# A two-layer convolution and linear-attention kernel: key tiles of 128 places in a row instead of every fourth column

## The chip, the cores and the metric

The kernel runs on one core of a Trainium2 chip. The metric is the time of one execution on the device in microseconds (us); the median of several runs is given. A core has five engines that each work through their own instructions in order and wait for each other through semaphores: TensorE (matrix products; in the profile PE for the matmuls and PEld for the loads of their stationary operand), VectorE (DVE), ScalarE (ACT), GpSimd (POOL) and SyncE (SP), which here issues all DMAs.

## The reference, cut to what matters

The input x has 16 batches of 256 channels, 64 rows and 64 columns, all in f32. Layer 0 adds to x a grouped 3x3 convolution of the normalized x, whose weights are rotated and modulated batch by batch. Layer 1 is linear attention over the N = 4096 places with a 5x5 depthwise convolution of v beside it:

```python
xt = x.reshape(B, C, N).transpose(0, 2, 1)
q = xt @ Wq.T + bq
kv = xt @ Wkv.T + bkv
k, v = (kv[..., :C], kv[..., C:])
...
z = 1.0 / (jnp.einsum('bic,bc->bi', q, k.sum(axis=1)) + 1e-06)
kv_state = jnp.einsum('bjc,bjd->bcd', k, v)
out = jnp.einsum('bic,bcd->bid', q, kv_state) * z[..., None]
fm = v.transpose(0, 2, 1).reshape(B * nh, hd, num, num)
fm = lax.conv_general_dilated(fm, dwc_w, window_strides=(1, 1), padding=[(KERNEL_SIZE // 2, KERNEL_SIZE // 2)] * 2, dimension_numbers=('NCHW', 'OIHW', 'NCHW'), feature_group_count=hd) + dwc_b[None, :, None, None]
```

Between these lines q and k are made positive, cubed and scaled back to their norm, place by place. The sums over j (all places) in `k.sum` and `kv_state` don't depend on the order of the places. The depthwise convolution does: it needs v by rows and columns.

## The kernel before

**Tiles.** After layer 0 a batch's x lies on chip as 8 tiles of 512 places (8 rows of 64), channels on partitions in two halves. The keys and values are made in 32 tiles of 128 places, places on partitions. A step n (`key_step`) makes tiles 2n and 2n+1; four tiles, two steps, share one tile of x. A product needs two matmuls, one for each half of the channels, and each f32 matmul of the program stands as two loads and two matmuls in the trace, so a tile has four and a step eight. Line 524 takes every fourth place of the 512 (`T % BC:CH:BC` with BC = 4 and CH = 512), that is, every fourth column of eight rows.

**From keys to state.** VectorE adds the bias (L493), takes the maximum with a small number (L494) and writes v into one of six buffers (L533). ScalarE squares the keys and sums the squares (L500), GpSimd cubes them (L503), ScalarE squares again, VectorE divides the two sums (`ratio`, L508 and L509), GpSimd takes the root (`root`, L512), and ScalarE scales the keys (`key_scale`, L544). `values` (L557) then multiplies keys and values into the state in small 128x32 products, 32 a key step. Step n calls ratio, root and key_scale for n-2, and every second step calls values for two earlier steps.

**v for the convolution.** `key_store` writes v of step n-1 at the end of step n into `vpad` in device memory. vpad has four planes, one for each column modulo 4; a plane holds, row by row, 16 columns of 256 numbers. `load_blocks` (L579) reads it back in an order that the depthwise product (L594) wants, 16 transfers for each half of the image: the first half in steps 7 to 14, the second during the attention. vpad is there twice, by even and odd batch.

**Order.** It is written out by hand (`tc.manual_schedule()`). For each batch come the key steps (the first three of a batch run inside the attention of the one before), then `between`, which starts the convolution of the next batch's layer 0 (`convolve`, L355, unit 0, whose rows `load_rows` fetched in step 11 as `xr`, L334 and L339), finishes the values and does the first half of the depthwise product, then 17 attention steps of 256 places. The preparation of a later batch's layer-0 weights (`prepare`, among it L266, L274, L286, L294) is handed out in pieces over the key steps. All DMAs go through SyncE in program order: stores and loads of v, xr, x for statistics (L97), weights and the output (L698). Eight semaphores tell of their landing, taken in turn.

**PSUM.** Six banks (`bank`) are shared by all products but the state's.

Of the kernel before, what the change touches and what calls it, by code (L numbers as in the profile page):

```python
# [15 lines left out]
P = 128  # L16
# [4 lines left out]
NH, HD = 8, 32  # L21
CH = 512
NCH = N // CH
NT = N // P
ROWS = CH // W
# [9 lines left out]
BR, BC = 8, 4  # L35
# [4 lines left out]
NV = 6  # L40
# [10 lines left out]
def conv_attention(ctx: ExitStack, tc: tile.TileContext, x, consts, kw, b1, w2, b2, b2r,  # L51
                   wkv, wq, brow, srow, wp, bp, dwb, band, out):
    nc = tc.nc
# [24 lines left out]
    def bank(name):  # L78
        return ps.tile([P, CH], F32, tag="bank", name=name)
# [4 lines left out]
    state = {}  # L84
# [57 lines left out]
    vbuf = []  # L142
# [254 lines left out]
    for name, src, bsrc in (("kv", wkv, brow[C:3 * C]), ("q", wq, brow[0:C])):  # L397
        n = src.shape[1]
        w = xp.tile([P, 2, n], F32, tag="x", name=f"wl{name}")
# [26 lines left out]
    for (w, br), lo in zip(wl.values(), (0, 2 * C)):  # L426
# [3 lines left out]
        n = w.shape[2]  # L430
# [11 lines left out]
    vpad = [dcp.tile([BC, H + 4, NJ, C], F32, tag=f"vpad{n}", name=f"vpad{n}") for n in range(2)]  # L442
# [45 lines left out]
    def focus(r, name):  # L488
        return {"r": r, "name": name, "s": sp.tile([P, 4, 2], F32, tag="s", name=f"s_{name}", bufs=5)}
# [24 lines left out]
    def key_products(b, n, j):  # L514

        w, _ = state[b]["kv"]
        if j == 0:
            r = rp.tile([P, 2, C], F32, tag="r0", name=f"rk_{b}_{n}", bufs=5)
            state[b]["k"][n] = focus(r, f"k_{b}_{n}")
            state[b]["k"][n]["pm"] = []  # L520
        T = 2 * n + j
        pm = bank(f"pk_{b}_{T}")
        for t in range(2):
            nc.tensor.matmul(pm, lhsT=state[b]["x"][n // 2][:, t, T % BC:CH:BC], rhs=w[:, t, :],  # L524
                             start=t == 0, stop=t == 1)
        state[b]["k"][n]["pm"].append(pm)

# [6 lines left out]

    def key_store(b, n):
        for j in range(2):
            k, y = (2 * n + j) % BC, ROWS * (n // 2) + 2
            nc.sync.dma_start(vpad[b % 2][k, y:y + ROWS].rearrange("y j n -> (y j) n"),
                              vbuf[n % NV][:, j, 0:HD, :].rearrange("p c h -> p (c h)"))

    def key_scale(b, n):
        f = state[b]["k"][n]
# [175 lines left out]
    def key_step(b, n, made):  # L718


        k = state[b]["k"]
        key_products(b, n, 0)
        if n >= 2:
            ratio(k[n - 2], False)
            root(k[n - 2])
        if n >= 1:
            squares(k[n - 1], 0)
            cube(k[n - 1])
        if n >= 2:
            key_scale(b, n - 2)  # L730
        key_bias(b, n, 0)
        next(made, None)
        key_products(b, n, 1)
        if n >= 1:
            squares(k[n - 1], 1)
        key_bias(b, n, 1)
        if n == LATE:
            values(b, 0)
        elif n > LATE and n % 2:
            values(b, n - LATE - 1)  # L740
            values(b, n - LATE)
        next(made, None)
# [40 lines left out]
    def attention_step(b, p, chain):  # L783
# [30 lines left out]
        if n >= 0:  # L814
            k = state[b + 1]["k"]
            key_products(b + 1, n, 0)
            key_products(b + 1, n, 1)
            if n == 2:
                ratio(k[0], False)
                root(k[0])  # L820
            if n >= 1:
                squares(k[n - 1], 0)
                cube(k[n - 1])
            key_bias(b + 1, n, 0)
            key_bias(b + 1, n, 1)
# [38 lines left out]
        if n >= 1:  # L864
            key_store(b + 1, n - 1)
# [7 lines left out]
    with tc.manual_schedule():  # L873
        fold_load(0, "q")
        made = iter(())
        for b in range(B):
            more = b + 1 < B
            state[b]["f"], state[b]["xq"] = {}, {}
            for n in range(0 if b == 0 else LEAD, NP):
                if b == 0 and n < 4:  # L880
                    load_stats(1, 2 * n)
                    load_stats(1, 2 * n + 1)
                if b == 0 and n == 4:
                    load_kernels(1)
                    made = prepare(1)
                key_step(b, n, made)
                if b == 0 and n < 4:
                    take_stats(1, 2 * n)
                    take_stats(1, 2 * n + 1)
                if n >= 1:  # L890
                    key_store(b, n - 1)
                if b > 0 and n == LEAD:
                    fold_load(b, "q")
                if n == 5:
                    fold_scale(b, "q")
                if n == 6:
                    fold_shift(b, "q")
                if 7 <= n < 15:
                    load_blocks(b, 2 * n - 14)
                    load_blocks(b, 2 * n - 13)  # L900
                if more and n == 11:
                    load_rows(b + 1, 0)
                if NP - 3 <= n < NP - 1:
                    blocked(b, n - NP + 3)
            key_store(b, NP - 1)
            for _ in made:
                pass
# [88 lines left out]
```

## Time and profile before

| what | value |
|---|---|
| median of 3 runs | 3578.64 us (3578.04 to 3583.35) |
| span of the profiled execution | 3572.8 us |
| VectorE, ScalarE, GpSimd busy | 66%, 56%, 45% |
| DMA moved in the span | 514.58 MB, 144 GB/s |
| DMA engines' time on SyncE's queue | 45.8% of 16 engines' span |
| granted TensorE clock, mean | 0.994 |

The span goes from the first to the last instruction of one profiled execution; a timed run has some microseconds around it. A row of the groups reads: line, engine, operation, what it writes and reads, shape, count, busy time in us, mean time of one in ns, and the idle time of the engine just before with what ended it. Busy time of a group counts overlapping instructions once, so it is less than count times mean for matmuls, which are pipelined; their ends are modelled, their starts are not. Idle time of an engine that doesn't set the pace costs nothing.

### The profile page before, as it was taken

To read this page: it belongs to the slowest core of one execution; us is meant where nothing else is said; L and a number is where in the kernel's file an instruction comes from. 1 tells how busy PE (TensorE), PEld (TensorE's weight loads), DVE (VectorE), ACT (ScalarE), POOL (GpSimd) and SP (SyncE) were. 2 spreads that over 40 slices of the span, in tenths; PEclk is the share of its full clock that TensorE was granted. 3 is DMA by queue.
4 is the path that set the end of the run, shared out by engine and by line. 5 is a ranking of instruction groups with operands and counts; after the bars stand their busy time and mean duration, and the time that the engine had idled before them with its cause. 6 is when DMAs were issued, how large, how long until landed. Compare 5 with 4: busy or idle time off the path is not lost. (4 is left out here: it accounts for less than half of the span.)

```text
span 3572.8 us, 114570 instructions
## 1 busy us (share of the span) xinstructions
PE 3457.5 (97%) x46568; PEld 2681.7 (75%) x46568; DVE 2341.4 (66%) x6627; ACT 2010.2 (56%) x6501; POOL 1623.0 (45%) x1807
## 2 busy tenths in 40 slices
PE   4899999999999999999999999999999999999999
PEld 3577787777877768777786877878778787877878
DVE  4656667666685666756666676666756667566656
ACT  2454655647555565655646546474555656556465
POOL 3344545445353453534545344454544535345445
PEclk9999999999999999999999999999999999999999
DMA  6353552635546254452645526355363544625242
GB/s 182 109 161 115 156 175 100 194 97 176 153 131 183 87 172 148 156 168 81 188 127 162 169 86 193 117 159 176 107 195 97 168 149 149 179 85 170 92 153 96
DMA packets 219857, 514.58 MB, mean 144 GB/s; under 512 B 26645, under 2 KB 99863, under 8 KB 207044
## 3 DMA queue, kind: packets, MB, share of 16 engines
q1 hardware_dynamic: 219332, 507.26, 45.8%
q8 instruction: 368, 6.03, 0.7%
q14 instruction: 157, 1.29, 0.1%
HBM read 371.63 MB, written 135.53 MB: 142 GB/s over the span
## 5 line engine op out<-in xcount | busy, mean ns | idle before, releaser
L524 PE MATMUL pk<-wkv,x 128*128 128x512 f32 x2048 | 957.4, 614 | 0.0
L662 POOL TENSOR_TENSOR o<-o,fm 128x256 f32<-128x256 f32 x512 | 362.1, 728 | 993.0 <-DVE o L660 852.0
L524 PEld LDWEIGHTS pk<-wkv,x 128*128 128x128 f32 x2048 | 616.1, 311 | 203.7 <-issue 2.8
L355 PE MATMUL pc<-xr,wt 32*32 32x504 f32 (+1 forms) x17856 | 623.7, 599 | 15.9 <-DMA xr<-in_x 8.6
L355 PEld LDWEIGHTS pc<-xr,wt 32*32 32x32 f32 x17856 | 387.8, 104 | 217.4 <-issue 101.7
L680 PE MATMUL py<-oT,wp 128*128 128x256 f32 x2048 | 505.9, 390 | 0.9 <-ACT oT L672 0.7
L619 PE MATMUL pq<-wq,xq 128*128 128x256 f32 x2048 | 489.6, 382 | 0.0
L500 ACT ACTIVATE r_k<-rk 128x256 f32<-128x256 f32 x1024 | 416.2, 408 | 112.4 <-POOL rk L503 69.0
L500 ACT ACTIVATE r_q<-rq 128x256 f32<-128x256 f32 x1024 | 413.7, 408 | 79.9 <-DVE rq L494 50.2
L368 ACT ACTIVATE x<-pc,shift 128x512 f32<-128x512 f32 x256 | 165.4, 690 | 442.3 <-PE pc L355 442.3
L680 PEld LDWEIGHTS py<-oT,wp 128*128 128x128 f32 x2048 | 370.0, 190 | 50.9 <-issue 3.6
L619 PEld LDWEIGHTS pq<-wq,xq 128*128 128x128 f32 x2048 | 370.8, 191 | 42.6
L544 ACT ACTIVATE rk<-rk,s_k 128x256 f32<-128x256 f32 x512 | 231.5, 499 | 253.9 <-POOL s_k L512 253.9
L493 DVE TENSOR_TENSOR pq<-pq,bq 128x512 f32<-128x512 f32 x256 | 177.2, 692 | 297.5 <-PE pq L619 297.3
L672 ACT COPY oT<-po 128x512 f32<-128x512 f32 x256 | 149.8, 585 | 391.9 <-PE po L670 391.4
L503 POOL TENSOR_TENSOR rk<-r_k,rk 128x512 f32<-128x512 f32 x256 | 327.5, 1279 | 70.5 <-ACT r_k L500 69.1
L512 POOL TENSOR_TENSOR s_k<-s_k,phalf 128x2 f32<-128x2 f32 x256 | 176.8, 691 | 388.9 <-DVE s_k L509 379.1
L503 POOL TENSOR_TENSOR rq<-r_q,rq 128x512 f32<-128x512 f32 x256 | 327.0, 1277 | 29.9 <-issue 28.1
L512 POOL TENSOR_TENSOR s_q<-s_q,phalf 128x2 f32<-128x2 f32 x256 | 178.9, 699 | 325.2 <-DVE s_q L509 262.4
L493 DVE TENSOR_TENSOR pk<-pk,bkv 128x256 f32<-128x256 f32 x512 | 218.1, 426 | 135.3 <-PE pk L524 133.5
L378 DVE TENSOR_TENSOR x<-x,shift 128x16 f32<-128x16 f32 x256 | 67.9, 265 | 324.0 <-ACT x L368 324.0
L651 PE MATMUL pn<-kvx,qT 128*128 128x132 f32 x2048 | 273.2, 277 | 0.0
(128 smaller groups left out, 5226.8 us busy)
## 6 DMA issues: line engine op xcount, KB each, us to landing
vh<-vpad SPq DMA_DIRECT2D x256, 384.0 KB
vh<-vpad SPq DMA_DIRECT2D x256, 360.0 KB
vpad<-v SPq DMA_DIRECT2D x512, 128.0 KB
out<-x SPq DMA_DIRECT2D x128, 512.0 KB
xr<-in_x SPq DMA_DIRECT2D x186, 320.0 KB
xs<-in_x SPq DMA_DIRECT2D x224, 256.0 KB
xr<-in_x SPq DMA_DIRECT2D x62, 288.0 KB
xs<-in_x SPq DMA_DIRECT2D x16, 512.0 KB
```

The lines of the kernel that those rows point to most:

```text
L355: nc.tensor.matmul(pcs[q].rearrange("p (r w) -> p r w", w=W)[ts(j, HD), :, to:to + n], lhsT=wt[ts(q, HD), j, k, :], rhs=g[ts(q, HD), j, r: ...
L368: nc.scalar.activation(state[b]["x"][i][:, t, :], state[b]["pc"][q], AF.Identity, bias=state[b]["shift"][:, t, 3:4])
L493: nc.vector.tensor_add(pm, pm, bias)
L500: nc.scalar.activation(f["r2"][:, j, :], f["r"][:, j, :], AF.Square, accum_out=f["s"][:, k, j:j + 1])
L503: nc.gpsimd.tensor_mul(f["r"], f["r2"], f["r"])
L512: nc.gpsimd.tensor_tensor(f["s"][:, 3, :], f["s"][:, 2, :], phalf, ALU.pow)
L524: nc.tensor.matmul(pm, lhsT=state[b]["x"][n // 2][:, t, T % BC:CH:BC], rhs=w[:, t, :], start=t == 0, stop=t == 1)
L544: nc.scalar.mul(f["r"][:, j, :], f["r"][:, j, :], f["s"][:, 3, j:j + 1])
L619: nc.tensor.matmul(pq[:, j, :], lhsT=xq[:, t, ts(j, P)], rhs=w[:, t, :], start=t == 0, stop=t == 1)
L651: nc.tensor.matmul(pn[:, :, 4 * hh:4 * hh + 4], lhsT=qT[:, hh, j, :], rhs=kvx[:, hh], start=True, stop=True)
L662: nc.gpsimd.tensor_add(o, o, fm[:, 2 * (m % NCH) + j, :])
L680: nc.tensor.matmul(py[:, co].rearrange("p y (J c) -> p J y c", c=BC), lhsT=wp_t[:, t, ts(co, P)], rhs=oT[:, t, :].rearrange("p (J y c) -> ...
```

## The change

A key tile becomes two whole rows of 64 places: tile T takes the places T % 4 times 128 to that plus 127 of its x tile, words in a row. A partition now stands for a column, the first 64 for one row and the other 64 for the next. So `key_store` writes each tile in two transfers, one a row of the image, from 64 partitions each; a row's 64 places go to the four planes in turn, 1 KB each. Before, a tile went to eight rows of one plane in one transfer from 128 partitions.

```diff
@@ key_products
         for t in range(2):
-            nc.tensor.matmul(pm, lhsT=state[b]["x"][n // 2][:, t, T % BC:CH:BC], rhs=w[:, t, :],
+            nc.tensor.matmul(pm, lhsT=state[b]["x"][n // 2][:, t, ts(T % 4, P)], rhs=w[:, t, :],
                              start=t == 0, stop=t == 1)
@@ key_store
         for j in range(2):
-            k, y = (2 * n + j) % BC, ROWS * (n // 2) + 2
-            nc.sync.dma_start(vpad[b % 2][k, y:y + ROWS].rearrange("y j n -> (y j) n"),
-                              vbuf[n % NV][:, j, 0:HD, :].rearrange("p c h -> p (c h)"))
+            for r in range(2):
+                y = 4 * n + 2 * j + r + 2
+                nc.sync.dma_start(vpad[b % 2][:, y].rearrange("k j n -> j k n"),
+                                  vbuf[n % NV][ts(r, W), j, 0:HD, :].rearrange("p c h -> p (c h)"))
```

`ts(i, n)` is the slice from i times n to (i + 1) times n. What vpad holds in the end is the same, and so is everything that reads it.

## The prediction

> **What bounds the kernel now.** I read the page first: busy time and the costliest groups.
>
> ```profile
> span 3572.8 us, 114570 instructions
> PE 3457.5 (97%) x46568; PEld 2681.7 (75%) x46568; DVE 2341.4 (66%) x6627; ACT 2010.2 (56%) x6501; POOL 1623.0 (45%) x1807
> ...
> L524 PE MATMUL pk<-wkv,x 128*128 128x512 f32 x2048 | 957.4, 614 | 0.0
> L524 PEld LDWEIGHTS pk<-wkv,x 128*128 128x128 f32 x2048 | 616.1, 311 | 203.7 <-issue 2.8
> ...
> L619 PEld LDWEIGHTS pq<-wq,xq 128*128 128x128 f32 x2048 | 370.8, 191 | 42.6
> ```
>
> TensorE is busy 97% of the span, and the key products (L524) are its largest group. Their weight load is the odd one: 311 ns, where the query product, a load of the same 128x128 f32, takes 191. The difference in the program is the step: L524 takes every fourth word of x, L619 words in a row. Whether those 120 ns cost time depends on what covers a load, so next comes TensorE's timeline in batch 1 (start, duration, matmuls merged).
>
> ```profile
> 348.94 0.60 PE L634 MATMUL pt<-consts,rq 128*128 128x128 f32 x4
> 349.38 3.72 PE L524 MATMUL pk<-wkv,x 128*128 128x512 f32 x8
> ...
> 376.25 1.21 PE L557 MATMUL pkv<-v,rk 128*32 128x33 f32 x64
> 377.39 3.82 PE L524 MATMUL pk<-wkv,x 128*128 128x512 f32 x8
> 381.05 1.03 PE L474 MATMUL pbq<-wq,co 128*128 128x256 f32 x4
> 381.91 3.61 PE L524 MATMUL pk<-wkv,x 128*128 128x512 f32 x8
> ...
> 434.09 2.00 PE L619 MATMUL pq<-wq,xq 128*128 128x256 f32 x8
> ...
> 470.79 1.89 PE L619 MATMUL pq<-wq,xq 128*128 128x256 f32 x8
> ```
>
> The same eight key matmuls take 3.61, 3.72 or 3.82 us, by what ran before them. Single starts in the trace say why. Inside a run they are 429 ns apart, and the 311 ns load hides fully under the matmul before. Only the first one of a run shows its load: its distance to the second is 657 ns after the small tiled products (L557, L294, L196, L209), 631 after L168 and L225, 550 after transposes (L634, L670), 443 after L474. So 228, 202, 121 and 14 ns are exposed. For the 191 ns load of the query the same two places show 104 ns after L557 (320 against 216; the 2.00 us row, whose forerunner is L557) and 2 ns after transposes (the 1.89 us row).
>
> **The weight load (L524).** It becomes 128 words in a row, as at L619. Its price is not in the trace for this line; the bounds are 311 (nothing gained) and nothing exposed at all, and I take L619's row, which has the same shape and type. Each entry then loses 228-104 = 124 ns after small products and 121-2 = 119 after transposes; after L168 and L225 I take 119 too, the difference of the loads. TensorE's order of instructions, which stays the same, has 220 runs of L524: 126 after small products, 30 after L168 and L225, 45 after transposes, 17 after L474, two others. Sum: 126 x 0.124 + 75 x 0.119 = 24.5 us of TensorE time. If nothing stayed exposed it would be 126 x 0.228 + 30 x 0.202 + 45 x 0.121 = 40.2 us. Inside the runs nothing changes.
>
> The Trainium skill (TensorE: Matmul & The Clock Gate, LDWEIGHTS (loading the stationary operand)) speaks against this: load time goes by the columns alone, 128 / 1.2 GHz, about 107 ns whatever the layout. By it the edit is worth nothing and the time stays at 3578.6. The rows of 311 and 191 ns for equal columns speak for another term, and I go by the rows.
>
> **How much of it reaches the end.** TensorE is not alone everywhere. I looked for places where it already waits, and found one in the key phase, here in batch 1 (TensorE, then ScalarE, then GpSimd).
>
> ```profile
> 410.82 1.50 PE L557 MATMUL pkv<-v,rk 128*32 128x33 f32 x64
> ```
> ```profile
> 410.91 0.91 ACT L544 ACTIVATE rk<-rk,s_k 128x256 f32<-128x256 f32 x2 [0.70 <-POOL s_k L512]
> ```
> ```profile
> 407.41 1.91 POOL L266 TENSOR_TENSOR rtmp<-mix,kw 128x864 f32<-128x864 f32 x1
> 409.27 0.84 POOL L333 COPY xr<-edge 32x256 f32<-32x256 f32 x2
> 410.19 0.69 POOL L512 TENSOR_TENSOR s_k<-s_k,phalf 128x2 f32<-128x2 f32 x1
> ```
>
> The group of values(9) and values(10) takes 1.50 us where others take 1.20, because key 10's scaled rows are just then being made: in 15 of 16 batches its matmuls start 0.10 us after ScalarE has finished them. The chain behind it is root (GpSimd), scaling and squares (ScalarE), ratio (VectorE), once a step, with the next batch's kernel preparation in between (L266, L333). It does not follow TensorE there: VectorE ends key tile 10 1.3 us after its last matmul, as it does wherever it waits for TensorE, but from tile 14 on 4.1 to 5.6 us after. What TensorE gains between tile 10 and values(10) is waited away at 410.82. That takes four entries in each of batches 1 to 14 (377.39, 386.58, 394.90, 403.63): 4 x 14 x 0.124 = 6.9 us. Batch 0 has a similar chain; I give it 0.4. Entries before tile 10 pull the chain along and are kept; after values(10) two more, 0.25 us, come before values(12), which has 0.3 us of room (0.4 us against the least, 0.1). Batch 15 prepares nothing, VectorE stays at 1.3 us, and all is kept.
>
> Kept: 24.5 - 6.9 - 0.4 = 17.2 us.
>
> **The stores (L534).** Two transfers of 128 KB a key step become four of 64 KB, 512 more on SyncE's queue. The packets stay at 1 KB and as many.
>
> ```profile
> L538 SPq DMA_DIRECT2D vpad<-v x512: 314/325/1470, 118.0 to 3462.0; - x171
> L579 SPq DMA_DIRECT2D vh<-vpad x512: 759/770/1567, 152.3 to 3504.4; - x171
> L448 SPq DMA_DIRECT2D vpad<-zero x16: 303/422/1307, 41.6 to 62.9; - x16
> ```
>
> An issue of the new shape is not in the trace. Bounds: 0.31 us (the least of L538) and 0.77 (L579); nearest is L448, which writes vpad in the same three-dimensional form, 0.42. A step of about 4.15 us then holds 4 x 0.42 + 2 x 0.77 = 3.2 us of issues, before 2 x 0.325 + 2 x 0.77 = 2.2. The queue still waits for VectorE's v, not the reverse. Behind the stores stand the loads of vh, xr and x. The program also gives DMAs eight semaphores in rotation, so each waits for the landing of the eighth before it, and with six a step instead of four that reaches less far back. From the landings around step 11 I estimate up to 1 us for that, so xr comes about 2 us late (1.04 us of issues, 1 of landings). Landing events in the trace put the last of unit 0's four xr 3.3 to 15.7 us (median 6.2) before its first matmul, and the last vh 7.0 us or more before the first-half depthwise. Less the roughly 1.1 us that TensorE gains until then, some 5 us of cover remain at the median and 2.2 at the tightest. Cost: 0. If the cover were gone, TensorE would stand in front of L355 with everything of `between` behind it.
>
> The Trainium skill (SBUF — State Buffer, Can I just issue two DMAs to hit both halves?) says that halves by partition serialize and one transfer of 128 is better. Doubling the stores' packet time by it (256 x 49 ns / 16 = 0.8 us a step) would raise the DMA share in the key phase from 0.72 to 0.91, still covered; the sum would not move.
>
> **VectorE's waits.** In the changed program 291 of the 512 writes of v (L533) wait for two DMAs instead of one, those of six steps earlier. Such a step is 25 us old and the slowest store landed after 12.3, so they don't block, but an extra wait instruction is 21 ns on VectorE. Queued behind it are the next tile's bias and the ratio. Bounds: 0, and 14 x 14 x 0.021 = 4.1 us if all between tile 11 and values(10) lie on the chain. I take 0: in the gating step VectorE itself waited 0.39 us for ScalarE.
>
> **Sum.** The profiled execution: 3572.8 - 17.2 = 3555.6 us of span. The median of the runs, 3578.64, lies 5.8 above that span; so 3561.4, say 3561.
>
> **Rivals.**
> A, everything kept: the chain at values(10) moves along with TensorE. 3578.6 - 24.5 = 3554. For it: TensorE's idle time put down to it is small; against: the same 0.10 us in 15 batches, and tile lags that only preparation explains.
> B, half kept: VectorE's extra waits lie on the chain (4.1 us), and xr is late in the tightest batches (some 2 us more): 3561 + 6 = 3567. The VectorE share of 89% (32.18 of 36 us between 385 and 421) speaks for it, its wait for ScalarE against.
> C, no gain: the load is long for another reason than its step, 3579. Against: L474, also beside 512-column matmuls of the same weights, loads in 191 ns.
> D, slower: the stores clog SyncE's queue, and xr comes late in all 15 batches. At 0.77 us a store, a step's issues are 6 x 0.77 = 4.6 us and the queue falls back 0.5 us a step, 2.5 us from step 7 to 11, about 5 with the step's own; that just uses up the cover. From a delay of 5 + 17.2 / 15 = 6.2 us on the kernel is slower than before; at 8 us it is 3561 + 15 x 3 = 3606. Against: L448's row.
>
> **How the numbers follow.** Forecast 0.65, A 0.12, B 0.09, C 0.06, D 0.08. The forecast's own range is 3557 to 3566. The range of 3552 to 3570 takes in A and B and leaves out C and D. From no change a measurement of this kernel can tell 0.2%, 7.2 us. Faster: forecast, A and B, 0.86; same: C, 0.06; slower: D, 0.08.
>
> **What would show it.** The load at L524 at about 191 ns; eight key matmuls after L557 in about 3.71 us, after transposes in 3.60; L557's group of values(10) longer than 1.50 us, at about 1.9 to 2.0, which shows A wrong; store issues near 0.42 us; no wait of L355 for xr at unit 0. A load still near 311 ns makes the whole forecast wrong; waits for xr or vh on TensorE mean D.

## The result, and the profile after

| kernel | median (runs) | ratio to before, 95% interval |
|---|---|---|
| before | 3582.27 us (6) | |
| changed | 3606.34 us (6) | 1.0049 [1.003, 1.0068] |

The change makes the kernel slower, by 0.49% (interval 0.3% to 0.68%) or 17.5 us; the medians above lie 24 us apart, at the upper end of that interval. The forecast was 17.2 us faster. The profiled execution has a span of 3609.5 us at a mean granted clock of 0.989. It is the slowest of its six runs, and the one profiled before (3572.8 us, to which a run's time adds 1.8 here) is quicker than all six of its kernel, so the two traces lie farther apart than the medians: 36.7 us. The lines of the page and of the groups that answer to those of before:

```profile
span 3609.5 us, 115334 instructions
PE 3454.2 (96%) x46568; PEld 2449.1 (68%) x46568; DVE 2343.7 (65%) x6627; ACT 2008.4 (56%) x6501; POOL 1621.3 (45%) x1807
...
L524 PE MATMUL pk<-wkv,x 128*128 128x512 f32 x2048 | 931.7, 601 | 0.0
...
L524 PEld LDWEIGHTS pk<-wkv,x 128*128 128x128 f32 x2048 | 373.9, 190 | 394.7 <-issue 374.8
...
L595 PE MATMUL pd<-vh,band 107*32 107x128 f32 x8192 | 255.0, 284 | 40.6 <-issue 40.5
```

The last line read, before:

```profile
L594 PE MATMUL pd<-vh,band 107*32 107x128 f32 x8192 | 240.2, 274 | 18.1 <-issue 17.8
```

The load of the key products fell from 311 to 190 ns, as forecast, and TensorE spends 25.7 us less on that line (957.4 before). Yet the span is 36.7 us longer, while TensorE's busy time is only 3.3 us shorter: the loss is idle time and, in the depthwise product (L595, L594 before), slower work, 255.0 us instead of 240.2. That line is the first hint: it has 40.6 us of idle time in front of its matmuls, ended by "issue", that is, by nothing that the profile shows. TensorE's wait view ranks such idle time (what waited, what for, us in all, times, longest):

```profile
PE pd L595 <- issue: 40.5, 28, 3.5
...
PE pkv L558 <- ACT rk L545: 13.2, 17, 1.3
PE pc L355 <- issue: 8.4, 8, 2.4
PE pc L355 <- DMA xr<-in_x: 7.1, 1, 7.1
```

Before, these were 17.8 (20 times, longest 2.1), 2.2, 7.3 and 8.6. No wait for xr has come up at the convolution, so rival D's mechanism did not happen; that its figure of 3606 is what was measured is chance.

I cut each batch at the starts of certain matmuls and summed the pieces over 16 batches, changed less before. Ahead of the first key tile: -2.1 us. From the first key tile to the last: -13.4. From there to the first-half depthwise: +9.9. Within the first-half depthwise: **+28.8**. Between the halves +5.0, within the second half +7.5, behind it +1.1. So the key phase gained nearly what it should, and one 7 us stretch a batch gave it all back and more. A second trace of the changed kernel ("changed, again" in the table below) has -13.0 in the key phase, +0.3 behind it and +37.4 in the first half: what the key phase gains is steady, the place of the loss varies by some 9 us from execution to execution. This is batch 7 in TensorE's timeline (start, duration, line, count, idle time before), changed and then before:

```profile
1757.41 2.16 PE L595 MATMUL pd<-vh,band 107*32 107x128 f32 x68
1759.82 3.69 PE L595 MATMUL pd<-vh,band 107*32 107x128 f32 x127 [0.25 <-issue]
1766.57 3.01 PE L595 MATMUL pd<-vh,band 107*32 107x128 f32 x61 [3.06 <-issue]
1769.51 1.11 PE L635 MATMUL pt<-consts,rq 128*128 128x128 f32 x4
```
```profile
1746.71 5.65 PE L594 MATMUL pd<-vh,band 107*32 107x128 f32 x199
1753.04 1.80 PE L594 MATMUL pd<-vh,band 107*32 107x128 f32 x57 [0.68 <-issue]
1754.77 0.66 PE L634 MATMUL pt<-consts,rq 128*128 128x128 f32 x4
```

A stall of 3.06 us stands in the middle of one stage, where the operands of all matmuls had long landed. And what follows it is slow as well: 61 matmuls take 3.01 us where 57 took 1.80 before, four transposes 1.11 instead of 0.66. SyncE's timeline shows what else had moved, again changed and then before:

```profile
1745.25 1.63 SPq L580 DMA_DIRECT2D vh<-vpad  x2
1746.98 7.18 SPq L539 DMA_DIRECT2D vpad<-v  x8
1754.27 1.02 SPq L97 DMA_DIRECT2D xs<-in_x  x2
1755.39 1.79 SPq L339 DMA_DIRECT2D xr<-in_x  x4
```
```profile
1735.90 0.88 SPq L97 DMA_DIRECT2D xs<-in_x  x2
1742.96 1.76 SPq L339 DMA_DIRECT2D xr<-in_x  x4
```

Before, SyncE had issued x (L97) 11 us ahead of the depthwise and then waited for the convolution of unit 0 to free the buffer of unit 1's xr. Now it issues stores without a pause, x comes 3 us ahead of the depthwise, and xr when the buffer has been free for 1.7 us. The windows view gives, for stretches of the depthwise, busy time of the engines, the granted clock, the share of the DMA engines and GB/s:

```profile
core 0: us, PE busy (x) PEld busy (x) DVE busy (x) ACT busy (x) POOL busy (x), PEclk, DMA share, GB/s
1757.40:1760.90 3.50, 3.25 (x117) 2.98 (x112) 3.29 (x10) 1.87 (x6) 0.00 (x0) 1.00 0.90 203
1760.90:1764.40 3.50, 2.61 (x95) 2.35 (x88) 1.41 (x5) 2.34 (x4) 1.81 (x2) 1.00 0.91 183
1764.40:1767.90 3.50, 1.33 (x40) 1.33 (x43) 0.00 (x0) 0.00 (x0) 0.11 (x1) 0.91 0.04 11
1767.90:1770.40 2.50, 2.50 (x33) 2.09 (x26) 0.00 (x0) 1.17 (x2) 0.00 (x0) 0.50 0.00 0
```

The first two stretches of the depthwise before, in the same view:

```profile
1746.70:1750.20 3.50, 3.50 (x142) 3.50 (x136) 3.29 (x10) 2.35 (x7) 0.00 (x0) 1.00 1.03 200
1750.20:1753.70 3.50, 2.82 (x104) 2.55 (x100) 1.47 (x5) 1.75 (x3) 1.75 (x2) 1.00 0.07 15
```

In the second stretch the DMA engines are still full (0.91); before, that stretch of this batch had a share of 0.07. The granted clock of 0.50 in the last one explains the slow matmuls behind the stall. The Trainium skill (TensorE: Matmul & The Clock Gate, Part 1: The HAM clock gate (the "warmup" mystery)) says that the clock falls to half after an idle stretch that fills an activity window of about 3.4 us; here one of 3.06 us was enough. In the clock records of this trace half clock comes in stretches of 3.41 us or a multiple of it, which fits the page's window, but from 439 us on it goes with stops of TensorE of 1.7 to 3.5 us.

What links full DMA engines to a TensorE without work? The page counts two queues for instructions; one of them, q8, has 368 packets of 16 KB, in both kernels. TensorE's 46568 loads and 46568 matmuls over 368 are 253 to a piece, so half of the depthwise, 256 matmuls and as many loads, is about two pieces. Around this stall the DMA view finds no piece from 1757.4 to 1763.9, and then, from 1763.9 to 1765.3 (packets, MB, share):

```profile
q8 instruction: 1, 0.02, 5.5%
```

It starts at 1763.96, takes 1.23 us, and TensorE goes on 1.38 us later. The theory: **TensorE's instructions are fetched by the same DMA engines as data; the depthwise, of small products, eats a piece every 3.6 us or so; and where the engines are full, the next piece is late and TensorE starves.**

### The profile page after: what moved, and what is told of

It reads as the page before. It is cut to its first block, busy times and chain, and to the rows that moved or that the text cites. A ratio compares the mean times of both kernels' runs of the same rounds, so it can differ in the third digit from the quotient of the medians.

```text
span 3609.5 us, 115334 instructions
## 1 busy us (share of the span) xinstructions
PE 3454.2 (96%) x46568; PEld 2449.1 (68%) x46568; DVE 2343.7 (65%) x6627; ACT 2008.4 (56%) x6501; POOL 1621.3 (45%) x1807
## 3 DMA queue, kind: packets, MB, share of 16 engines
q1 hardware_dynamic: 227524, 507.30, 46.4%
## 5 line engine op out<-in xcount | busy, mean ns | idle before, releaser
L524 PE MATMUL pk<-wkv,x 128*128 128x512 f32 x2048 | 931.7, 601 | 0.0
L524 PEld LDWEIGHTS pk<-wkv,x 128*128 128x128 f32 x2048 | 373.9, 190 | 394.7 <-issue 374.8
L355 PE MATMUL pc<-xr,wt 32*32 32x504 f32 (+1 forms) x17856 | 623.5, 598 | 15.5 <-issue 8.4
L355 PEld LDWEIGHTS pc<-xr,wt 32*32 32x32 f32 x17856 | 382.2, 103 | 222.4 <-issue 106.3
L493 DVE TENSOR_TENSOR pk<-pk,bkv 128x256 f32<-128x256 f32 x512 | 218.3, 426 | 119.3 <-PE pk L524 118.7
L595 PE MATMUL pd<-vh,band 107*32 107x128 f32 x8192 | 255.0, 284 | 40.6 <-issue 40.5
L595 PEld LDWEIGHTS pd<-vh,band 107*32 107x32 f32 x8192 | 236.9, 114 | 55.1 <-issue 52.7
```

The source lines that it names most:

```text
L355: nc.tensor.matmul(pcs[q].rearrange("p (r w) -> p r w", w=W)[ts(j, HD), :, to:to + n], lhsT=wt[ts(q, HD), j, k, :], rhs=g[ts(q, HD), j, r: ...
L493: nc.vector.tensor_add(pm, pm, bias)
L524: nc.tensor.matmul(pm, lhsT=state[b]["x"][n // 2][:, t, ts(T % 4, P)], rhs=w[:, t, :], start=t == 0, stop=t == 1)
L595: nc.tensor.matmul(pd[ts(j, HD), k, :].rearrange("p (R m h) -> p R m h", R=4, m=4), lhsT=band_t[:, c + k, :], rhs=vb[:, :, :, j, c + k, :] ...
```

## The experiments

Ratios are to the kernel before, run on the same chip. The table sums the time from the first to the last matmul of each half of the depthwise over 16 batches, gives the DMA engines' share in the second 3.5 us of the first half (mean of the 15 batches with loads behind them), and TensorE's "issue" waits at the depthwise. Each row is one trace; the two of the changed kernel differ by 8.7 us in the first half, so a smaller difference between kernels there says little:

| kernel | ratio, 95% interval | first half | second half | DMA share | "issue" |
|---|---|---|---|---|---|
| before | 1 | 137.0 | 112.5 | 0.06 | 17.8 |
| changed | 1.0049 [1.003, 1.0068] | 165.8 | 120.0 | 0.53 | 40.5 |
| changed, again | 1.0052 [1.0032, 1.0072] | 174.5 | 115.5 | 0.65 | 43.8 |
| products alone | 0.9972 [0.9956, 0.9987] | 143.9 | 115.7 | 0.08 | 24.1 |
| stores alone | 1.0082 [1.006, 1.0104] | 174.2 | 114.1 | 0.57 | 43.1 |
| changed, one store a tile | 0.9966 [0.9949, 0.9983] | 149.1 | 122.4 | 0.09 | 30.7 |
| before, two plain stores | 1.0073 [1.0048, 1.0098] | 166.1 | 118.0 | 0.63 | 42.9 |
| changed, unit 1's rows later | 0.9977 [0.9965, 0.9989] | 112.4 | 132.1 | 0.02 | 11.5 |
| one store, unit 1's rows later | 0.9968 [0.9954, 0.9983] | 110.8 | 130.4 | 0.02 | 11.9 |
| before, unit 1's rows later | 1.000 [0.9979, 1.002] | 110.8 | 130.0 | 0.02 | 13.0 |
| changed, last stores later | 1.0032 [1.002, 1.0045] | 154.7 | 119.3 | 0.40 | 32.1 |
| one store, both rows later | 0.9854 [0.9832, 0.9877] | 110.8 | 110.8 | 0.02 | 0.0 |

### The two halves of the change

Products alone:

```diff
-lhsT=state[b]["x"][n // 2][:, t, T % BC:CH:BC]
+lhsT=state[b]["x"][n // 2][:, t, ts(T % 4, P)]
```

> Only the weight load's layout is changed (128 places in a row); the stores of v are those of the kernel before, so v's rows stand at wrong places in vpad and the first-half depthwise reads them so; all work has its size. Theory (products gain, stores lose): L524 PEld about 190 ns, the segments of the key phase shorter by about 15 us in sum, depthwise as before (L594 PE about 240 us, its issue stalls about 18 us): 3582 - 15 = about 3566 us. Rival (the products' gain never reaches the end, or the new layout itself causes the loss in the depthwise): 3582 or above, with depthwise stalls as in the changed kernel.

Stores alone: line 524 of before with `key_store` of the change.

> Only the stores are changed (four transfers of 64 partitions a step, into both halves of the planes); the products are those of the kernel before, so v's rows stand at wrong places in vpad. Theory (SyncE's queue runs late with stores of some 0.59 us each; x and four xr transfers fall into the first-half depthwise, where the fetch of TensorE's instructions then comes late): before + 40, about 3622 us, with stalls of 2 to 3.5 us in the depthwise (L595) that show 'issue', about 40 us of them in sum, and the clock below full speed behind them. Rival (the loss needs the new layout of the products, or TensorE's earlier arrival): 3582, depthwise as before.

Measured: 0.9972, 10 us faster, and 1.0082, 29 us slower. The sum, 19 us, is the change's 17.5 within its interval (11 to 24 us): as far as that tells, the halves act apart from each other. The new layout of the products is not to blame. Yet the products gave 10 us and not 15, and the stores cost 29 and not 40. Here is the constant that speaks for the theory: in the six traces so far (with the next two kernels), two neighbouring depthwise matmuls start more than 0.9 us apart in 93 places, from 0.95 to 4.41 us (one matmul takes 0.27), and every one of these gaps ends 1.21 to 1.72 us after an instruction piece has landed. Before has 9 of them, changed 17.

### One transfer or two, this form or that

```diff
-            for r in range(2):
-                y = 4 * n + 2 * j + r + 2
-                nc.sync.dma_start(vpad[b % 2][:, y].rearrange("k j n -> j k n"),
-                                  vbuf[n % NV][ts(r, W), j, 0:HD, :].rearrange("p c h -> p (c h)"))
+            y = 4 * n + 2 * j + 2
+            nc.sync.dma_start(vpad[b % 2][:, y:y + 2].rearrange("k y j n -> (y j) k n"),
+                              vbuf[n % NV][:, j, 0:HD, :].rearrange("p c h -> p (c h)"))
```

> The changed kernel with one transfer of 128 partitions a tile instead of two of 64 (same bytes, same 1 KB rows, both rows of the picture in one, destination in three dimensions). Theory: two stores a step, at most 0.6 us each, leave SyncE 2 x 0.6 + 2 x 0.8 = 2.8 of 4.15 us, so the queue is on time, the depthwise stalls go, and the products' gain of about 15 us stays: about 3566 us. Rival (the loss comes from where the rows of v are written in vpad, or from the new layout): still about 3600.

And the kernel before, its store split without a new form:

```diff
-            nc.sync.dma_start(vpad[b % 2][k, y:y + ROWS].rearrange("y j n -> (y j) n"),
-                              vbuf[n % NV][:, j, 0:HD, :].rearrange("p c h -> p (c h)"))
+            for r in range(2):
+                z = y + 4 * r
+                nc.sync.dma_start(vpad[b % 2][k, z:z + 4].rearrange("y j n -> (y j) n"),
+                                  vbuf[n % NV][ts(r, W), j, 0:HD, :].rearrange("p c h -> p (c h)"))
```

> The kernel before, each store split into two halves of 64 partitions that each fill one stretch of 64 KB in one plane: the number of transfers of the changed kernel without its three-dimensional destination. Theory has two branches: if the form sets the issue time, each issue takes 0.31 to 0.35 us, a step 4 x 0.33 + 2 x 0.8 = 2.9 us, SyncE is on time and the time is 3582 to 3588; if an issue of 64 partitions is long whatever its form (0.5 us and more), the queue is late and the time rises as with the stores alone, to about 3620.

Measured: 0.9966 and 1.0073. With one transfer a tile the loss is gone, although v lands where the change puts it (the stalls, expected to go, are not: 30.7 us in the table); with two it is there, although nothing else has changed. The stores' issues by line (shortest, median, longest in ns), of changed, one store and two plain stores:

```profile
L539 SPq DMA_DIRECT2D vpad<-v x1024: 517/588/2207, 115.3 to 3500.6; - x171
```
```profile
L538 SPq DMA_DIRECT2D vpad<-v x512: 517/557/1744, 117.9 to 3470.1; - x171
```
```profile
L540 SPq DMA_DIRECT2D vpad<-v x1024: 445/590/1967, 116.8 to 3505.3; - x171
```

An issue of 64 rows takes 0.59 us in either form, that of 128 rows 0.56 in the new form and 0.325 in the old. Issues on SyncE sum to 948 us before, 1396 changed, 1052 with one store, 1378 with two plain ones. The loss goes with this sum, so with the number of transfers, and not with where the rows go. Nor did the moving itself become dearer: packets of SyncE's queue took 46.4% of the 16 engines' time in the changed kernel and 45.8% before.

### Unit 1's rows behind the depthwise

```diff
@@ between
-        if more:
-            load_rows(b + 1, 1)
@@ attention_step, behind load_blocks
+        if more and p == 1:
+            load_rows(b + 1, 1)
```

> The changed kernel with the four xr loads of unit 1 (1.28 MB a batch) issued behind step 1's loads of vh, which wait for the first-half depthwise, instead of before it. In all six traces so far each stall of over 0.9 us within the depthwise ends 1.2 to 1.7 us after a 16 KB piece of the queue of instructions has landed. Theory (the pieces come late behind SyncE's late transfers): the stalls of the first-half depthwise go from about 48 us in sum to under 15, and the time falls by 25 to 35 us against the changed kernel, to 3570 to 3580. Rival (the pieces are late for another reason, such as the number of transfers itself): stalls stay near 48 us, time near 3605. A wait of unit 1's products (L355) for xr may come up; it would show by name.

> One transfer of 128 partitions a tile, and unit 1's xr loads behind the first-half depthwise: the contiguous products with both causes of late instruction pieces taken away. Theory: stalls in the depthwise below 15 us (31 with the one store alone), so 15 to 20 us below that kernel, about 0.9915 of the kernel before. Rival: as with the one store alone, 0.9966.

> The kernel before with only unit 1's xr loads moved behind the first-half depthwise. Theory: the stalls that the kernel before has itself (22.8 us in 19 gaps) mostly go, 12 to 20 us faster, 0.995 of the kernel before. Rival (stalls have nothing to do with these transfers): 1.000.

For the changed kernel the theory holds: 1.0049 becomes 0.9977, some 26 us, and the first half falls to 112.4 us, with 110.8 in the other two; 16 x 6.9 us is what it takes without a stall. The windows view of batch 7 of the kernel before with the rows moved, both stretches of its depthwise:

```profile
core 0: us, PE busy (x) PEld busy (x) DVE busy (x) ACT busy (x) POOL busy (x), PEclk, DMA share, GB/s
1737.50:1741.00 3.50, 3.50 (x144) 3.50 (x137) 3.29 (x10) 2.32 (x7) 0.00 (x0) 1.00 0.02 5
1741.00:1744.50 3.50, 3.50 (x140) 3.47 (x128) 1.51 (x5) 2.37 (x5) 1.71 (x2) 1.00 0.02 5
```

With idle DMA engines (0.02) TensorE is busy without a break. But the other two expectations failed: 0.9968 where 0.9915 was expected, 1.000 where 0.995. The loss had moved. In the kernel before with the rows moved, the first half gains 26.2 us, the second half loses 17.5 and the stretch between them 16.1, of which the waits at the convolution, 4.7 us more than before, are the part that the wait view shows (before: 17.8 and 7.3):

```profile
PE pd L594 <- issue: 13.0, 10, 3.4
PE pc L355 <- issue: 12.0, 11, 1.9
```

### Provoking it in the kernel before

Two more transfers a tile with next to no bytes, and three more of 428 KB behind unit 1's xr:

```diff
+            for r in range(2):
+                nc.sync.dma_start(dump[b % 2, n, j, r], vbuf[n % NV][ts(r, W), j, 0, 0:1])
```
```diff
         if more:
             load_rows(b + 1, 1)
+            for q in range(3):
+                nc.sync.dma_start(dump[q], band_t)
```

> The kernel before with two more transfers a tile, each of 64 rows of 4 bytes into a scratch tensor that nobody reads: more issues, next to no more bytes. Theory (SyncE's issue time makes its queue late): if such an issue costs 0.4 us or more, a step holds 2 x 0.33 + 4 x 0.4 + 2 x 0.8 = 3.9 us and more, SyncE is late as in the changed kernel, and the depthwise stalls rise to 40 to 50 us, time 25 to 30 us above before. Rival (what counts is how the 64-partition transfers spread over the DMA engines, not the issues): time within 5 us of before.

> The kernel before with three transfers of 428 KB a batch (a constant tile written to a scratch tensor that nobody reads) behind unit 1's xr, so that 1.28 MB more are under way during the first-half depthwise. Stores, products and their issues are those of before. Theory (transfers under way in the depthwise delay the pieces of TensorE's instructions): first-half depthwise up from 136 us to 150 or more over 16 batches, stalls with 'issue' in the wait view up from 17.8 us by 10 to 40 us, time 10 to 40 us above before. Rival (it takes the many small issues of the stores): depthwise and time as before, within 5 us.

Both overshot, at 1.2026 [1.2004, 1.2049] and 1.1299 [1.1273, 1.1325], and prove nothing for either side. Their wait views:

```profile
PE pc L355 <- DMA xr<-in_x: 313.2, 18, 25.4
PE pd L597 <- DMA vh<-vpad: 65.1, 5, 29.8
PE pd L597 <- issue: 42.7, 38, 3.1
```
```profile
PE pt L635 <- POOL rq L504: 361.7, 14, 27.1
PE pd L595 <- issue: 42.7, 29, 3.5
```

The small rows made SyncE's queue so late that TensorE stood in front of L355 for xr, 313 us of it: this is rival D's mechanism, and shows how it would have looked in the changed kernel. In the other kernel SyncE stood 8.5 and 17.2 us in issuing the second and third added transfer, they took 39 us to land (median), and what came behind was held up; the first half stayed at 143.9 us, below the 150 expected, and the second half rose from 112.5 to 144.5. "issue" rose in both from 17.8 to 42.7.

### The last stores behind the loads

```diff
@@ between
         if more:
             load_rows(b + 1, 1)
+        key_store(b, NP - 2)
+        key_store(b, NP - 1)
```

The two calls stood ahead of `between` before.

> The changed kernel with the eight stores of the last two key steps (14 and 15; the second-half depthwise needs them, the first does not) issued behind x and unit 1's xr instead of before them. The number of transfers, their form and every other place stay. Theory (what costs is that the late queue pushes x and xr into the first-half depthwise): about 8 x 0.59 = 4.7 us less stands before xr, so xr lands up to 4.7 us earlier, most of it ahead of the depthwise; first-half depthwise sums to 130 to 145 us over 16 batches (165 in the changed kernel, 136 before, 110 without any stall), time 10 to 25 us below the changed kernel. Rival (the count of transfers itself, or the later transfers, set the loss): within 5 us of the changed kernel.

> The changed kernel once more, unaltered, as the measure for the run with the last stores later on the same chip: 1.005 of before, first-half depthwise about 165 us over 16 batches.

1.0032 against 1.0052 in the same company: 7 us better where 10 to 25 were expected, with intervals that overlap ([1.002, 1.0045] and [1.0032, 1.0072]), first half 154.7 where 130 to 145 were. x and xr came earlier, but the moved stores now ran in the depthwise themselves: a share of 0.40 in its second stretch, between 0.06 and 0.65, and its time lies between too. That fits a loss that goes by how full the engines are and not by whose transfers fill them; alone it does not show it.

### Both loads of rows behind the depthwise

Unit 3's rows, issued in step 8 right ahead of the second half, go to step 10:

```diff
-        if u and u < 3:
-            load_rows(b + 1, u + 1)
+        if u == 1:
+            load_rows(b + 1, 2)
 ...
             store(b, p - 3)
+        if more and p == 10:
+            load_rows(b + 1, 3)
```

> One transfer of 128 partitions a tile, unit 1's xr behind the first-half depthwise and unit 3's xr behind the second-half depthwise (step 10 instead of 8). Theory: both halves of the depthwise near 6.9 us in every batch; if the stalls don't turn up at the convolution (L355) instead, 10 us below the kernel with unit 1's rows alone moved, about 0.994 of before. Rival (stalls move on to the next stretch that reads instructions fast): 0.997, with 'issue' at L355 above 15 us.

Measured: 0.9854, 50 us and more below the kernel before and faster than either kernel. Both halves stand at 110.8 us, and the group of the depthwise has no idle time left; the convolution's "issue" waits stay small:

```profile
L594 PE MATMUL pd<-vh,band 107*32 107x128 f32 x8192 | 230.3, 273 | 0.0
```
```profile
PE pc L355 <- issue: 9.2, 11, 1.9
```

So the stalls did not move on this time, which the forecast of 10 us below the kernel with unit 1's rows alone had understated. Without stalls the halves of the change can be weighed afresh:

> The changed kernel, two transfers of 64 partitions a tile, with unit 1's xr behind the first-half and unit 3's xr behind the second-half depthwise. Theory (the stores cost only by what they push into the depthwise): within 5 us of the kernel with one store a tile and both rows moved, 0.985 to 0.988 of before, both halves at 111 to 116 us over 16 batches. Rival (late stores cost by themselves too, by vh or x): 10 us and more above it, 0.989 or more, with waits for vh or x by name.

> The kernel before with both loads of xr moved, nothing else. With no stalls in the way the products' gain must show whole against the kernel with one store a tile and both rows moved: theory (the sum over the key phases, 17.2 us predicted, 13 to 15 measured from the traces): 13 to 17 us above that kernel, 0.9895 of before. Rival (only 10 us, as in the products alone): 0.988.

These gave 0.9893 [0.9876, 0.991], with halves of 113.5 and 110.8 us, and 0.9912 [0.9896, 0.9928]. So the halves came as the theory has them, the changed kernel's time as the rival has it. As the one-store kernel had run on another chip, the three were put side by side:

> One store a tile, contiguous products, both xr loads moved, beside the next two on one chip. By the profiles (3544.6 against 3553.6 us of span): about 9 us below the kernel before with both loads moved. By the forecast's sum: 17 us below it.

> The changed kernel with both xr loads moved. By the profiles (3546.3 against 3544.6): within 4 us of the kernel with one store. If late stores cost by themselves: 10 us and more above it.

> The kernel before with both xr loads moved, the measure for the two others: about 0.990 of before.

| both rows later, on one chip | median | ratio, 95% interval |
|---|---|---|
| contiguous products, one store a tile | 3538.76 us | 0.9846 [0.9827, 0.9866] |
| changed | 3549.55 us | 0.9874 [0.9857, 0.9891] |
| before | 3554.34 us | 0.9891 [0.9875, 0.9907] |

The products with one store are worth 15.6 us by the medians, near the forecast's 17 and not the 9 that two profiles suggested. The stores of 64 partitions cost 10.8 us even here, though their interval overlaps the other's, and leave the whole change a gain of 4.8 us, which these intervals cannot tell from none. The profiles put the 10.8 us in three places, 3.9 us ahead of the first half, 6.3 between the halves and 6.6 behind the second, but the earlier pair of profiles of the same two kernels has 0.3, -3.0 and about 3 there, and no wait names a cause. That part stays open.

## Why the prediction was wrong, point by point

**The weight load was right.** 190 ns against 191 forecast. Eight key matmuls take 3.70 us after L558 (3.71 forecast) and 3.60 after transposes (3.60):

```profile
345.94 0.60 PE L635 MATMUL pt<-consts,rq 128*128 128x128 f32 x4
346.38 3.60 PE L524 MATMUL pk<-wkv,x 128*128 128x512 f32 x8
...
372.53 1.21 PE L558 MATMUL pkv<-v,rk 128*32 128x33 f32 x64
373.67 3.70 PE L524 MATMUL pk<-wkv,x 128*128 128x512 f32 x8
```

The first of a run is now 533 ns from the second after small products, 104 more than the 429 within a run, as at the query; after L168 and L225 it is 512, after transposes 432. That is 124 and 119 ns less than before, as taken. The Trainium skill's rule that a load's time goes by its columns alone (TensorE: Matmul & The Clock Gate, LDWEIGHTS (loading the stationary operand)), an estimate of 107 ns here, fits neither kernel: 311 and 190 ns for equal columns.

**The part lost at values(10) was right in kind, somewhat too small.** TensorE's timeline of batch 1:

```profile
390.92 7.13 PE L524 MATMUL pk<-wkv,x 128*128 128x512 f32 x16
397.98 1.27 PE L558 MATMUL pkv<-v,rk 128*32 128x33 f32 x64
...
406.66 0.69 PE L558 MATMUL pkv<-v,rk 128*32 128x33 f32 x32
408.09 0.84 PE L558 MATMUL pkv<-v,rk 128*32 128x33 f32 x32 [0.74 <-ACT rk L545]
```

TensorE waits 0.74 us for ScalarE's scaled key 10; from the first group's start to the second's end are 2.27 us, a little over the 1.9 to 2.0 forecast (1.50 before), and values(8), at 1.27 instead of 1.20, begins to feel it too. The stretch from tile 10 to values(10) got longer by 1.9 us over all batches instead of keeping its length. In TensorE's waits for the scaled keys (2.2 us before, 13.2 now, above) the loss reads 11.0 us, where 6.9 + 0.4 were forecast. The measured gain is 13.4 us between the first and the last key tile, against 17.2 for the whole; the first entry of each batch, 16 x 0.12 = 1.9 us, lies ahead of that stretch. Rival A falls with this.

**VectorE's second wait cost nothing, as taken.** With single waits (products alone) that stretch lengthened by 2.6 us, no less than the 1.9 with both.

**The stores are the step that failed, twice.** First the price: 0.42 us an issue, from L448, where 0.588 was measured; the bounds of 0.31 and 0.77 held, but the row chosen as nearest was not near. A step then needs 4 x 0.588 + 2 x 0.795 = 3.9 us of 4.15 on SyncE, instead of 3.2, and stores longer than the median make it late (the eight of 7.18 us above took 0.9 each with the pauses between them). The rest of the forecast's delay, 1 us of waits for earlier landings, did not show: in the 33 us before the depthwise of batch 7 SyncE waited 3.5 us for landings, 5.2 before the change. Nor did the doubled packet time that the prediction weighed: the DMA share of that stretch of the key phase in batch 1 is 0.69 (0.72 before). Second, and this decided, the cover. "Cost: 0" was argued from what waits for a transfer: xr of unit 0 at L355 and vh. Those margins held; no such wait arose. Left out was what the late transfers run beside, which the sum had at nothing and which measured +28.8 us in the first half alone. SyncE's slack before the depthwise had emptied the DMA engines for the second part of that stage, and TensorE's instructions need them there. The forecast looked at the queue behind the stores as far as xr of unit 0, and not at x and unit 1's xr, which no engine was waiting for.

**Rival D had the place of the cause (SyncE's queue) and the wrong victim.** L355 waited 7.1 us for xr, once, in the first batch, as before.

That TensorE's stalls were instruction pieces in want of DMA engines rests on four findings: the constant 1.2 to 1.7 us from a piece's landing to the next matmul; the table's DMA share and first half, which rise together (with one kernel out of order, the two plain stores: 0.63, but 166.1 us); the vanishing of the stalls when the engines are idle; and the delay itself. The delay shows when the pieces are numbered in the changed kernel's trace and in that of the changed kernel with both rows moved, the last one taken, where the same matmuls come in the same order but for four of 46568. Of the pieces that start within the first halves of 15 batches, 15 start behind 1.5 us in which the engines were over 80% busy, and by then TensorE has begun 34 to 117 matmuls more (median 68) than when the same piece started in the other trace; for the 14 that start behind engines under 10% busy the median is about 10. The piece of batch 7 above is 87 matmuls late; at 27 ns a matmul that is about 2.4 us. What sets the moment at which a piece is asked for was not seen, nor why, with only unit 1's rows moved, the second half stalls more than before.

## What to carry to other kernels

A transfer that no engine waits for can still cost time: ask which stage it will run beside, and whether that stage is made of many short matmuls. In this kernel an "issue" wait within a run of such matmuls, full DMA engines and a late packet on the instruction queue belonged together, and loads moved behind both halves of the stage cured it, for 0.9 to 1.1% of the kernel before's time with no other edit. Splitting a DMA in two did more here than double its count: two issues of half the rows cost 1.18 us where one cost 0.325.

## What the runs showed of the hardware that was not expected

- TensorE's instructions come in 16 KB pieces over the DMA engines (368 pieces, 0.9 to 1.9 us each in the changed kernel). The depthwise of 6.9 us needs one every 3.6 us or so; a late one stopped TensorE for up to 3.5 us in the changed kernel, 4.1 with the stores alone.
- After such a stop of 3.06 us the granted clock was 0.50 for 3.41 us, which added to the loss.
- The issue of a store of 64 rows of 1 KB took 0.59 us, whether its destination was one stretch of memory or four planes; that of 128 rows 0.325 us into one plane and 0.557 into four. Why half the rows take longer than the whole stays open.
- 64 rows of 4 bytes a transfer, two more a tile, slowed the kernel by 20%.
